# A grouped 3x3 convolution: building the even output bank by accumulation and the odd one from a copy taken in between

## The chip, the cores and the metric

The kernel runs on one core of a Trainium2 chip. Its time is the device time of one execution in microseconds, the median over several runs. Beside it stands one execution recorded by the hardware profiler, from which all views of the profile come. The engines are written as in the profile: PE is TensorE (matrix products; its weight loads are listed apart as PEld), DVE is VectorE, ACT is ScalarE, POOL is GpSimd, SP is the queue that issues most DMAs.

## The reference

The input x has 160 images of 128 channels and 32 x 32 positions. Each image is group-normalised (32 groups of 4 channels), convolved with a 3x3 kernel of 128 x 128 channels, and added to itself. There are five sets of weights; 32 images use each. The weights are U quantised on two levels with steps taken from the range of the whole of U.

```python
beta, alpha = jnp.max(U), jnp.min(U)
s1 = (beta - alpha) / 3.0
v1 = s1 * floor(U / s1)
s2 = s1 / 5.0
v2 = s2 * floor((U - v1) / s2)
w = (v1 + v2).reshape(OUT_CH * 5, IN_CH, 3, 3)
# x viewed as (32, 5 * 128, 32, 32), five groups, padding 1
out = x + conv(group_norm(x), w, feature_group_count=5)
```

## The kernel before

**The arithmetic.** An output image is held as two PSUM banks of 128 x 512 values, called even and odd: for most purposes the even and the odd rows (or, in images called combined, the even and the odd columns). Two neighbouring outputs of a three-tap filter share work: with taps g0, g1, g2, one product of g0+g1+g2 with a sum of the two inner inputs, and one product of g0-g1+g2 with their difference; half the sum and half the difference of these two products are the shared parts of the two outputs. So an image needs four groups of products: SUM weights with the sums (quarter 2 of the prepared input), DIFF weights with the differences (quarter 3), and one group each with the outer taps for the even and the odd bank (quarters 0 and 1). Inputs are fp16, split into a high and a low part for accuracy. A *combined* image has all quarters in both parts (tiles `vh` and `vl`, 128 x 2048, 24 products of up to 512 columns). Another image takes its high part by the plain taps (18 products of tile `hi`) and only its low part by quarters (tile `rows`, 12 products). `combined` decides which image is of which kind: every second one up to image 29, then three of five, then three of four.

**The path of one image through the engines.** `sums_of_pairs` (L854) lets PE make the DIFF products in the bank `m2_ps` and the SUM products in `m1a` or `m1b`. `leave` (L888, its instruction is L891) lets ACT copy half of `m2_ps` to SBUF, tile `m`. `pairs` (L894) lets DVE write the even bank as half of m1 plus m (L903), and the odd bank as half of m1 minus m (L905). `main` (L878) lets PE add the remaining products to the even bank (a = 0) and to the odd bank (a = 1). `residual` (L921) then copies both banks, in one ACT instruction of 1024 columns (L929), to a tile `sum`, which a DMA of POOL's queue adds to the output in memory (L953). The first three and the last four images are finished by DVE instead (L946).

**What is prepared ahead.** ACT measures each image in two passes (L241, L248; eight images are measured by DVE), makes `vh` (L738) or `hi` (L648), and for some images `z` (L640). DVE makes `vl` (L744) or `lo` and `rows` (L751, L764, L772, L773), and in `combine` a part of the tile `v` (L690, L697). POOL makes the rest of `v` (L678, L708) or `z` (L714); `beside_pairs` ties its start to an instruction of DVE in the same step, so that it runs beside `pairs`. The weights of the next set are quantised on DVE in small pieces (class `Later`, L142 to L162, L549) strewn between these.

**The order.** Everything is ordered by hand, in `run`: a program of 160 steps, in which each engine's instructions are queued in the order of the calls. In step i, `conv(i)` queues on PE `sums_of_pairs(i + 1)`, then `main(i, 0)` and `main(i, 1)`. ACT gets: the first pass of new measurements, `residual(i - 1)`, `leave(i + 1)`, the high part of an image further on, the second pass. DVE gets: the low part of image i+2 (from step 14 on of image i+3; in step 13 both images 15 and 16), `pairs(i + 1)`, `combine` of image i+4 (later i+5), measurements. Images 0 to 2 are done by plain taps; step 3 (`FIRST`) is the first of the regular ones. `FURTHER` is 11.

**PSUM.** [...] two pairs for even and odd (`ps_eo`), `m1a`, `m1b`, `m2_ps`, and one for small things.

## Time and profile before

| | |
|---|---|
| median of three runs | 966.45 us (965.62 to 966.77) |
| the profiled execution, its time | 964.56 us |
| its span, first to last instruction | 962.5 us |
| PE busy | 927.8 us, 4432 products |
| DVE busy | 902.6 us |
| ACT busy | 862.7 us |
| POOL busy | 460.1 us |
| mean granted PE clock | 0.995 |

The profiled execution took 2.1 us more than its span, and 1.9 us less than the median. "Busy" is the time in which at least one instruction of the engine was under way. Rows of the view by line give the count, the busy time, the mean duration of one instruction, and after the second bar the idle time of the engine just before these instructions with what ended it. The mean duration of a product (375 ns) is longer than the spacing of products, which overlap; from the starts in the timeline, a product of 512 columns follows the one before after 0.21 us. The page's chain of work that ended last is empty for this run, so that the waits have to be read from the view of waits and the timeline.

### The profile page before, as it was taken

The numbers are of one execution on the slowest core, as the hardware profiler recorded it, in microseconds if no ns is written. First come the engines' busy times: TensorE is split into PE (matmuls) and PEld (weight loads), VectorE is DVE, ScalarE is ACT, GpSimd is POOL, SyncE is SP. The second block draws the span as 40 slices with busy tenths as digits, with TensorE's granted clock in tenths as the row PEclk, the third lists the DMA queues.
The fourth block names the chain that finished last, engine by engine and source line by source line (L and its number), as shares of the span: only waits on it lengthen the run. The fifth ranks groups of instructions, "written<-read, shape, count | busy, mean of one in ns | idle before, by whom it ended". The sixth has DMA issues, their size and how long they took to land.

```text
span 962.5 us, 13034 instructions
## 1 busy us (share of the span) xinstructions
PE 927.8 (96%) x4432; PEld 433.8 (45%) x4432; DVE 902.6 (94%) x1269; ACT 862.7 (90%) x1167; POOL 460.1 (48%) x477
## 2 busy tenths in 40 slices
PE   2899989999999999999999999999999999999997
PEld 1344434444444444444444444444444444444443
DVE  7989999999899999989999999899999998999993
ACT  5879989999899999999999999999999999997660
POOL 4344434456445445554545445545444366565640
PEclk9999999999999999999999999999999999999999
DMA  9079999999999999999999999999999999856563
GB/s 349 36 267 345 334 348 320 325 321 325 328 321 323 317 295 308 272 306 254 295 251 289 284 293 297 282 277 286 267 273 267 282 279 269 172 91 107 91 107 112
DMA packets 67450, 254.22 MB, mean 264 GB/s; under 512 B 5296, under 2 KB 5296, under 8 KB 67376
## 3 DMA queue, kind: packets, MB, share of 16 engines
q1 hardware_dynamic: 45344, 173.09, 48.0%
q0 software_dynamic: 22032, 80.23, 44.4%
q8 instruction: 36, 0.59, 0.2%
q14 instruction: 38, 0.31, 0.1%
HBM read 89.19 MB, written 164.10 MB: 263 GB/s over the span
## 4 chain that ended last, share of the span: by engine, by line


## 5 line engine op out<-in xcount | busy, mean ns | idle before, releaser
L788 PE MATMUL eo<-hi,wt 128*128 128x496 f16 (+3 forms) x1170 | 310.8, 376 | 2.4 <-DVE eo L905 1.7
L843 PEld LDWEIGHTS <-wt 128*128 128x128 f16 x1884 | 183.9, 99 | 211.5 <-DVE eo L905 2.7
L744 DVE SCALAR_TENSOR_TENSOR vl<-v,rstd,vh 128x2048 f16<-128x2048 f32 x94 | 221.8, 2360 | 0.2 <-ACT vh L738 0.2
L843 PE MATMUL eo<-vh,wt 128*128 128x512 f16 x561 | 210.1, 375 | 1.2 <-DVE eo L905 1.2
L843 PE MATMUL eo<-vl,wt 128*128 128x512 f16 x561 | 210.1, 374 | 0.0
L738 ACT ACTIVATE vh<-v,rstd 128x2048 f16<-128x2048 f32 x94 | 188.2, 2002 | 4.8 <-DVE v L697 4.3
L929 ACT COPY sum<-eo 128x1024 f32<-128x1024 f32 x153 | 161.0, 1052 | 32.3 <-PE eo L843 31.7
L788 PEld LDWEIGHTS <-wt 128*128 128x128 f16 x1242 | 121.2, 99 | 142.8 <-DVE eo L905 4.9
L678 POOL TENSOR_SCALAR v<-xt,ngm 128x64 f32<-128x64 f32 x94 | 79.1, 842 | 202.0 <-DVE vl L744 86.9
L248 ACT ACTIVATE junk<-xt,mv 128x1024 uint8<-128x1024 f32 x152 | 174.4, 1148 | 0.3
L241 ACT ACTIVATE junk<-xt 128x1024 uint8<-128x1024 f32 x152 | 160.5, 1056 | 13.3 <-DMA xt<-in_x_dram 10.0
L714 POOL TENSOR_SCALAR z<-xt,ngm,rstd 128x1024 f32<-128x1024 f32 x49 | 93.3, 1904 | 165.1 <-DVE rows L773 55.0
L843 PEld LDWEIGHTS <-across 128*128 128x128 f16 x1128 | 110.8, 98 | 131.9 <-issue 4.9
L843 PE MATMUL eo<-rows,wt 128*128 128x512 f16 x378 | 143.5, 380 | 0.0
L953 POOL DMA_DIRECT2D out_dram<-sum x153 | 133.7, 874 | 14.4 <-ACT sum L929 6.6
L690 DVE TENSOR_TENSOR v<-xt 128x960 f32<-128x960 f32 x94 | 114.0, 1212 | 0.0
L843 PE MATMUL m<-vl,across 128*128 128x496 f16 (+1 forms) x282 | 106.4, 377 | 2.1 <-DVE vl L744 2.1
L891 ACT ACTIVATE m<-m 128x512 f32<-128x512 f32 x157 | 93.7, 597 | 14.1 <-PE m L843 13.7
L843 PE MATMUL m<-vh,across 128*128 128x496 f16 (+1 forms) x282 | 106.2, 376 | 0.2 <-ACT m L891 0.2
L708 POOL TENSOR_TENSOR v<-xt 128x512 f32<-128x512 f32 x94 | 97.2, 1034 | 0.0
L751 DVE TENSOR_TENSOR lo<-z,hi 128x1024 f16<-128x1024 f32 x66 | 80.6, 1221 | 0.0
L286 POOL TENSOR_TENSOR rstd<-ve,mhalf 128x8 f32<-128x8 f32 (+2 forms) x24 | 42.3, 1761 | 65.1 <-DVE rows L773 21.1
(150 smaller groups left out, 1166.3 us busy)
## 6 DMA issues: line engine op xcount, KB each, us to landing
xt<-in_x_dram SPq DMA_DIRECT2D x78, 1024.0 KB, 9.6
out_dram<-sum POOLq DMA_DIRECT2D x153, 512.0 KB, 8.7
out_dram<-xt SPq DMA_DIRECT2D x76, 1024.0 KB, 14.2
out_dram<-xt SPq DMA_DIRECT2D x7, 512.0 KB, 3.3
u<-in_L_conv_U_dram SPq DMA_DIRECT2D x4, 576.0 KB, 13.6
xt<-in_x_dram SPq DMA_DIRECT2D x4, 512.0 KB, 10.1
range<-in_L_conv_U_dram SPq DMA_DIRECT2D x3, 576.0 KB, 8.3
u<-in_L_conv_U_dram SPq DMA_DIRECT2D x2, 288.0 KB, 3.1
```

Source lines behind the costliest of these rows:

```text
L241: self.nc.scalar.activation(junk, image, ACTF.Copy, scale=-1.0 / image.shape[1], accum_out=self.mv[:, j, 0:1],)
L248: self.nc.scalar.activation(junk, image, ACTF.Square, bias=self.mv[:, j, 0:1], accum_out=self.mv[:, j, 1:2],)
L690: nc.vector.tensor_tensor(self.view(v, 1, (511, 2), (half, H), (1, half - 1)), self.view(x, 1, (1, 2), (W, H), (2, half - 1)), self.view(x ...
L708: ins = nc.gpsimd.tensor_sub(self.v[i][:, 1536:], odd, even)
L714: ins = nc.gpsimd.tensor_scalar(z, self.image(i), st.ngm[:, j], st.rstd[:, j], ALU.add, ALU.mult)
L738: self.nc.scalar.mul(vh, self.v[i], st.rstd[:, j])
L744: yield self.nc.vector.scalar_tensor_tensor(vl, self.v[i], st.rstd[:, j], self.hi[i], ALU.mult, ALU.subtract)
L788: nc.tensor.matmul(self.bank(target, a)[:, first:end, c0:c1], self.wts[n, col][:, k, :], tile[:, s0 : s0 + 2 * (end - first) - 1 : 2, c0 + ...
L843: self.nc.tensor.matmul(out, weights, moving, start=start and j == 0, stop=False, skip_group_check=True)
L891: self.nc.scalar.mul(m2, self.m2_ps, 0.5)
L929: nc.scalar.copy(self.as_banks(i, self.sum[i]), self.flat(i, eo))
L953: added = self.nc.gpsimd.dma_start(self.ov[n, :, b], self.sum.pop(i), accum_op=ALU.add)
```

## The change

The four pieces of an output pair are put together in another way. PE makes the SUM products directly in the image's even bank (`begin`). ACT copies that bank to SBUF, tile `half` (`leave`, now L906, a plain copy). PE then adds the DIFF products to the same bank (`complete`), which so becomes the sum of both. DVE makes the odd bank alone: twice the copy minus the even bank (`odd_from_even`, L913). For the factors to fit, SUM and DIFF weights are halved when they are made (one more instruction each time), and LIFT, a scale that weights and inputs share, is halved.

Even and odd banks come from pools of their own, four and three banks; m1a, m1b and m2_ps are gone. `residual` copies the two banks with two ACT instructions of 512 columns (L941), and in the images finished by DVE adds them with two instructions (L955).

The order of the calls changes too. In the steady steps (from step 15) PE's queue is `complete(i + 1)`, `begin(i + 2)`, `main(i, 0)`, `main(i, 1)`, and ACT gets `leave(i + 2)` at the place where it had `leave(i + 1)`. In steps 4 to 14 PE's queue is `begin(i + 1)`, `main(i, 0)`, `complete(i + 1)`, `main(i, 1)`, and ACT gets `leave(i + 1)` ahead of all else in the step. In step 14 `begin(16)` and a second `leave` come in addition. In step 3 `complete(4)` comes last; `complete(3)` stands behind the last plain taps of step 2, just ahead of `main(3, 0)`. The numbers of products are the same as before. `main(i, 0)` adds to the bank that `odd_from_even(i)` reads, so it waits for that instruction, as it waited for `pairs(i)`.

```diff
-LIFT = 2.0**14
+LIFT = 2.0**13
...
-        self.ps_eo = pool("ps_eo", 2, space=PSUM)
-        ps_m = pool("ps_m", 1, space=PSUM)
+        self.ps_even = pool("ps_even", 4, space=PSUM)
+        self.ps_odd = pool("ps_odd", 3, space=PSUM)
...
         yield engine.tensor_tensor(total, g0, g2, ALU.add)
+        yield engine.tensor_tensor(total, total, g1, ALU.add)
+        yield engine.tensor_scalar_mul(total, total, 0.5)
         yield engine.tensor_tensor(diff, total, g1, ALU.subtract)
-        yield engine.tensor_tensor(total, total, g1, ALU.add)
...
-    def sums_of_pairs(self, i):
-
-        for quarter, kind, target in (
-            (3, self.DIFF, self.m2_ps), (2, self.SUM, self.m1(i))
-        ):
-            for step in self.KS:
-                self.product(target, i, quarter, step, kind, start=step == self.KS[0])
+    def begin(self, i):
+
+        even = self.bank_of(self.ps_even, i)
+        self.eo[i] = [even]
+        for step in self.KS:
+            self.product(even, i, 2, step, self.SUM, start=step == self.KS[0])
+
+    def complete(self, i):
+
+        for step in self.KS:
+            self.product(self.eo[i][0], i, 3, step, self.DIFF)
+
+    def steady(self, i):
+
+        return i > self.FURTHER + 2
...
-        if self.FIRST < i < self.imgs - 1:
-            self.sums_of_pairs(i + 1)
-        if i == self.FIRST:
+        ahead = range(i + 1, self.imgs)[:1]
+        if self.steady(i) and self.steady(i - 1):
+            for k in ahead:
+                self.complete(k)
+            for k in range(i + 2, self.imgs)[:1]:
+                self.begin(k)
+            self.main(i, 0, lambda: on_the_way(self.COLS[1]))
+            self.main(i, 1, lambda: on_the_way(self.COLS[2]))
+        elif i == self.FIRST:
             self.main(i, 0)
-            self.sums_of_pairs(i + 1)
+            self.begin(i + 1)
             on_the_way(self.COLS[1])
             self.main(i, 1)
             on_the_way(self.COLS[2])
+            self.leave(i + 1)
+            self.complete(i + 1)
         else:
+            self.begin(i + 1)
             self.main(i, 0, lambda: on_the_way(self.COLS[1]))
+            self.leave(i + 1)
+            self.complete(i + 1)
+            if self.steady(i):
+                self.begin(i + 2)
             self.main(i, 1, lambda: on_the_way(self.COLS[2]))
...
-        m2 = self.evac.tile([self.P, self.H // 2, self.W], F32, tag="m2", name=f"m2_{i}")
-        self.nc.scalar.mul(m2, self.m2_ps, 0.5)
-        self.m2[i] = m2
+        half = self.half[i] = self.evac.tile(
+            [self.P, self.H // 2, self.W], F32, tag="half", name=f"half{i}"
+        )
+        self.nc.scalar.copy(half, self.eo[i][0])
...
-        nc.vector.scalar_tensor_tensor(even, m1, 0.5, m2, ALU.mult, ALU.add)
-        between()
-        nc.vector.scalar_tensor_tensor(odd, m1, 0.5, m2, ALU.mult, ALU.subtract)
+        even, odd = self.eo[i][0], self.bank_of(self.ps_odd, i)
+        self.eo[i].append(odd)
+        self.nc.vector.scalar_tensor_tensor(
+            odd, self.half.pop(i), 2.0, even, ALU.mult, ALU.subtract
+        )
...
-            nc.scalar.copy(self.as_banks(i, self.sum[i]), self.flat(i, eo))
+            image = self.as_banks(i, self.sum[i])
+            for a in range(2):
+                nc.scalar.copy(image[:, a], self.flat(i, eo[a]))
...
                 if i == self.FIRST - 1:
-                    self.sums_of_pairs(self.FIRST)
+                    self.begin(self.FIRST)
+                    self.leave(self.FIRST)
...
+                if i == self.FIRST - 1:
+                    self.complete(self.FIRST)
...
-                if i + 1 < self.imgs:
-                    self.leave(i + 1)
+                if self.steady(i) and i + 2 < self.imgs:
+                    self.leave(i + 2)
...
                 if i + 1 < self.imgs:
-                    self.pairs(i + 1)
+                    self.odd_from_even(i + 1)
```

More of the change, by code (lines that the diff above doesn't have):

```diff
@@ L455, in __init__ @@
         self.small = pool("small", 3)
-        self.ps_eo = pool("ps_eo", 2, space=PSUM)
-        ps_m = pool("ps_m", 1, space=PSUM)
+        self.ps_even = pool("ps_even", 4, space=PSUM)
+        self.ps_odd = pool("ps_odd", 3, space=PSUM)
         ps_small = pool("ps_small", 1, space=PSUM)
         self.steps = Steps(nc, keep)
-        self.m1a, self.m1b, self.m2_ps = (
-            ps_m.tile([P, self.H // 2, self.W], F32, tag=name, name=name)
-            for name in ("m1a", "m1b", "m2")
-        )
-        self.pair = [self.m1a, self.m2_ps]
         small = ps_small.tile([P, 512], F32, tag="small", name="small")
         self.pt, self.pg = small[:, : ROW * P].rearrange("p (k o) -> p k o", k=ROW), small[:, ROW * P :]
-        self.chunks, self.z, self.hi, self.v, self.eo, self.m2 = {}, {}, {}, {}, {}, {}
+        self.chunks, self.z, self.hi, self.v, self.eo, self.half = {}, {}, {}, {}, {}, {}
         self.sum, self.stored = {}, {}
         self.tables, self.wts, self.across = {}, {}, {}
-        self.columns = []
+        self.columns, self.warm = [], None
         cuts = [0, 2, 4, 8, 12, 16, 20, *range(24, self.imgs + 1, 8)]
@@ L524, in over_partitions @@
         nc, P = self.nc, self.P
-        place = self.bank_pair("range").rearrange("p h r w -> p h (r w)")
-        rows = place[0:1, 0, : 2 * P].rearrange("p (k c) -> p k c", k=2)
+        place = [self.bank_of(pool, "range").rearrange("p r w -> p (r w)") for pool in (self.ps_even, self.ps_odd)]
+        rows = place[0][0:1, : 2 * P].rearrange("p (k c) -> p k c", k=2)
         for k in range(2):
@@ L532, in over_partitions @@
         nc.vector.tensor_reduce(top, rows, AX.X, ALU.max)
-        spread = place[:, 1, :2]
+        spread = place[1][:, :2]
         nc.tensor.matmul(spread, self.ones, top, start=True, stop=True)
@@ L788, in taps @@
                 nc.tensor.matmul(
-                    self.bank(target, a)[:, first:end, c0:c1],
+                    target[a][:, first:end, c0:c1],
                     self.wts[n, col][:, k, :],
@@ L795, in taps, with bank_of @@
                 )
-    def bank_pair(self, i):
-        return self.ps_eo.tile([self.P, 2, self.H // 2, self.W], F32, tag="eo", name=f"eo{i}")
-    def bank(self, target, h):
-        return target[h] if isinstance(target, list) else target[:, h]
+    def bank_of(self, pool, name):
+        tag = "even" if pool is self.ps_even else "odd"
+        return pool.tile([self.P, self.H // 2, self.W], F32, tag=tag, name=f"{tag}{name}")
     def warm_up(self, count):
         zeros = self.los[3].rearrange("p h w -> p (h w)")
+        if self.warm is None:
+            self.warm = self.bank_of(self.ps_odd, "warm")
         for _ in range(count):
             self.nc.tensor.matmul(
-                self.pair[0].rearrange("p i w -> p (i w)"), zeros[:, :128],
+                self.warm.rearrange("p i w -> p (i w)"), zeros[:, :128],
                 zeros[:, :512], start=True, stop=True,
@@ L815, in direct_hi @@
         if i not in self.eo:
-            self.eo[i] = self.bank_pair(i) if i < 2 else self.pair
+            self.eo[i] = [self.bank_of(pool, i) for pool in (self.ps_even, self.ps_odd)]
         self.taps(i, (self.hi[i], 0), col, self.eo[i])
@@ L845, in product @@
             )
-    def m1(self, i):
-        return self.m1b if i % 2 else self.m1a
     def both(self, i):
         return ([self.hi[i]] if self.combined(i) else []) + [self.v[i]]
-    def sums_of_pairs(self, i):
-        for quarter, kind, target in (
-            (3, self.DIFF, self.m2_ps), (2, self.SUM, self.m1(i))
-        ):
-            for step in self.KS:
-                self.product(target, i, quarter, step, kind, start=step == self.KS[0])
-    def conv(self, i, on_the_way):
-        if self.FIRST < i < self.imgs - 1:
-            self.sums_of_pairs(i + 1)
-        if i == self.FIRST:
+    def begin(self, i):
[8 more added lines that the diff above has]
+        return i > self.FURTHER + 2
+    def conv(self, i, on_the_way):
+        ahead = range(i + 1, self.imgs)[:1]
[7 more added lines that the diff above has]
+        elif i == self.FIRST:
             self.main(i, 0)
-            self.sums_of_pairs(i + 1)
+            self.begin(i + 1)
             on_the_way(self.COLS[1])
@@ L878, in main @@
     def main(self, i, a, between=lambda: None):
-        to = self.bank(self.eo[i], a)
+        to = self.eo[i][a]
         for step in self.KS:
@@ L888, in leave, with odd_from_even @@
     def leave(self, i):
-        m2 = self.evac.tile([self.P, self.H // 2, self.W], F32, tag="m2", name=f"m2_{i}")
-        self.nc.scalar.mul(m2, self.m2_ps, 0.5)
-        self.m2[i] = m2
-    def pairs(self, i, between=lambda: None):
-        nc = self.nc
-        m1, m2 = self.m1(i), self.m2.pop(i)
-        eo = self.eo[i] = self.bank_pair(i)
-        if i == self.imgs - 1:
-            eo = self.eo[i] = [eo[:, 0], self.m1(i - 1)]
-        even, odd = (self.bank(eo, a) for a in range(2))
-        nc.vector.scalar_tensor_tensor(even, m1, 0.5, m2, ALU.mult, ALU.add)
-        between()
-        nc.vector.scalar_tensor_tensor(odd, m1, 0.5, m2, ALU.mult, ALU.subtract)
+        half = self.half[i] = self.evac.tile(
+            [self.P, self.H // 2, self.W], F32, tag="half", name=f"half{i}"
+        )
+        self.nc.scalar.copy(half, self.eo[i][0])
+    def odd_from_even(self, i):
+        even, odd = self.eo[i][0], self.bank_of(self.ps_odd, i)
[3 more added lines that the diff above has]
+        )
     def as_banks(self, i, image):
@@ L911, in as_banks, with flat @@
         return image.rearrange("p (i a w) -> p a i w", a=2, w=self.W)
-    def flat(self, i, banks):
-        return banks.rearrange("p a i w -> p a (i w)") if self.combined(i) else banks
+    def flat(self, i, bank):
+        return bank.rearrange("p i w -> p (i w)") if self.combined(i) else bank
     def by_hand(self, i):
@@ L941, in residual @@
         image = self.as_banks(i, xj)
-        if eo is self.pair:
-            for a in range(2):
-                nc.vector.tensor_add(image[:, a], self.bank(eo, a), image[:, a])
-        else:
-            nc.vector.tensor_add(image, self.flat(i, eo), image)
+        for a in range(2):
+            nc.vector.tensor_add(image[:, a], self.flat(i, eo[a]), image[:, a])
         self.store(i)
@@ L1027, in run @@
             self.measure(i)
-        first_means = self.bank_pair("means").rearrange("p h r w -> p h (r w)")
+        first_means = [self.bank_of(pool, "means").rearrange("p r w -> p (r w)") for pool in (self.ps_even, self.ps_odd)]
         spread = self.over_partitions(
-            ext1, ident, lambda: self.stats_of(0).means(first_means[:, 0])
+            ext1, ident, lambda: self.stats_of(0).means(first_means[0])
         )
@@ L1064, in run @@
         measure(1, 3)
-        self.stats[1].means(first_means[:, 1])
+        self.stats[1].means(first_means[1])
         self.stats[1].deviations()
@@ L1173, in run @@
                 if i == 2:
-                    self.leave(3)
                     self.normalise(5)
@@ L1177, in run @@
                     self.high_part(5)
-                    self.pairs(3)
+                    self.odd_from_even(3)
                     self.low_part(4)
```

## The prediction, made before the changed kernel ran

> **What bounds the kernel now.** I began with the engines' totals on the page and the busy time in stretches of 40 us (columns: stretch, then busy us and count for PE, PEld, DVE, ACT, POOL, then granted clock, DMA share, GB/s).

> ```profile
> PE 927.8 (96%) x4432; PEld 433.8 (45%) x4432; DVE 902.6 (94%) x1269; ACT 862.7 (90%) x1167; POOL 460.1 (48%) x477
> ```

> ```profile
> 80.00:120.00 40.00, 40.00 (x199) 19.33 (x198) 39.39 (x67) 38.52 (x56) 15.12 (x17) 1.00 1.04 333
> 120.00:160.00 40.00, 36.05 (x161) 15.79 (x160) 39.55 (x64) 36.27 (x50) 13.38 (x15) 0.96 1.04 337
> 160.00:200.00 40.00, 40.00 (x194) 18.85 (x193) 39.66 (x57) 37.54 (x54) 20.20 (x25) 1.00 1.05 325
> 320.00:360.00 40.00, 40.00 (x195) 18.82 (x193) 38.48 (x53) 39.72 (x55) 18.59 (x18) 1.00 1.05 309
> 840.00:880.00 40.00, 40.00 (x192) 18.68 (x191) 38.17 (x41) 39.70 (x53) 23.23 (x22) 1.00 0.63 99
> ```

> About 194 products per 40 us are one per 0.206 us. Only 120:160 falls short, with 161. So PE's stream sets the time, and only its halts can be won. The waits of PE, and the timeline around the greatest, show them (time, duration, engine, instruction; in brackets idle time before it and who ended it):

> ```profile
> PE m L843 <- DVE vl L744: 2.1, 1, 2.1
> PE eo L788 <- DVE eo L905: 1.7, 2, 1.0
> PE eo L843 <- DVE eo L905: 1.2, 3, 0.5
> PE m L843 <- DVE rows L773: 0.8, 1, 0.8
> PE m L843 <- ACT m L891: 0.2, 1, 0.2
> ```

> ```profile
> 127.43 0.38 PE L843 MATMUL m<-vh,across 128*128 128x512 f16 x1 [0.19 <-ACT m L891]
> 129.88 0.59 PE L843 MATMUL m<-vl,across 128*128 128x512 f16 x1 [2.08 <-DVE vl L744]
> ...
> 131.09 0.62 PE L843 MATMUL m<-vh,across 128*128 128x496 f16 x1
> ...
> 131.50 0.62 PE L843 MATMUL m<-vl,across 128*128 128x496 f16 x1
> ...
> 134.63 0.81 PE L788 MATMUL eo<-hi,wt 128*128 128x512 f16 x3 [0.70 <-DVE eo L905]
> ```

> Here PE waits for DVE's `vl`, goes on at half rate, and waits again for the odd bank of image 14. From 126.86 to 134.63, 7.77 us, it starts 13 products, which take 2.8 us elsewhere: 5.0 us are lost. Read in the same way after 55 us: 0.9 at 65.9 (low part late), 0.4 before that, 1.1 at 157.4, 0.4 at 268, 0.6 at 495, 0.7 at 722, 0.2 at 772 (odd bank late). Sum 9.3, of which 9.0 wait for DVE or follow from it. The first 55 us and the end, from 955 us, are not touched by the change.

> [...] 131.09 to 131.50 is 0.41 us, and the lines above end 3.4 us later at full rate. So two microseconds of halt can cost 1.7 us more. [...]

> **The change, part by part.** The groups by line, shapes apart:

> ```profile
> L929 ACT COPY sum<-eo 128x1024 f32<-128x1024 f32 x153 | 161.0, 1052 | 32.3 <-PE eo L843 31.7
> L891 ACT ACTIVATE m<-m 128x512 f32<-128x512 f32 x157 | 93.7, 597 | 14.1 <-PE m L843 13.7
> L903 DVE SCALAR_TENSOR_TENSOR eo<-m1b,m 128x512 f32<-128x512 f32 x79 | 54.7, 692 | 16.4 <-PE m1b L843 11.9 <-ACT m L891 4.5
> L905 DVE SCALAR_TENSOR_TENSOR eo<-m1b,m 128x512 f32<-128x512 f32 x78 | 54.5, 699 | 2.7
> ```

> PE: both programs have the same TensorE instructions in number and size. Nothing.

> DVE loses one of two instructions per image: 157 x 0.73 (the spacing of L903 and L905) = 115 us of busy time. Taken from an engine that isn't the bound, it is worth only the halts that DVE causes. The new operand places (SBUF and PSUM read, PSUM written) are those of L903; I take its 0.70.

> ACT's `leave` stays at 0.60. The residual's copy becomes two: by mean durations 2 x 597 - 1052 = 142 ns more, 22 us in all; by spacing (L891 to the next start 0.485 us, L929 0.96) 0.01 us, 1.5 us in all. Back to back, spacing counts; I take 0.01. ACT has 32.3 + 14.1 us idle before these very lines, which hides it; without that cover, where ACT is at 39.7 of 40, it would be up to 0.14 per image. Seven additions by DVE are split likewise and hidden. The halving of weights is 8 more DVE pieces of some 0.35 us (L573's size) and four on POOL, which delay the first `z` by 0.2 us beside PE's taps: nothing. LIFT: nothing.

> Steady steps, from 15 on. `main(i, 0)` waits for `odd_from_even(i)` where it waited for `pairs(i)`, and DVE gets there 0.7 us sooner. The five halts at 157 and later (1.1, 0.4, 0.6, 0.7, 0.2) are each close to or below that, and `odd_from_even` needn't wait for `leave` of its own step. Gain 3.0. `begin(i + 2)` needs the low part a step sooner than before, but DVE makes it ahead of the odd bank that the next `main` waits for anyway. `leave` must end before the next step's `complete`, the same deadline as before for m2_ps; there one wait of 0.2 is seen. It can start 0.6 to 1.3 us later, since `begin` now follows `complete`; then ACT's idle time before L891 grows. DVE's odd bank stands behind it, with a step to spare.

> Steps 3 to 14, where 6.3 us are lost today. Here I walked along the queues with the rows' durations (a product group 0.64, or 1.28 if combined; half a main 2.55, or 1.27):
> - `main(3, 0)` follows `complete(3)` at once, and the odd bank lies between: 0.27 for the end of the product to be seen (942.24 to 943.16 less three spacings), 0.70, 0.06. One halt of 1.0, new; behind it on DVE stands low part 4, which `begin(4)` needs. Low parts 4 and 5 end about as late as today.
> - `leave(i + 1)` stands first in ACT's step, so it can't run ahead with measurements while `begin` is under way. In step 9 ACT has two images to measure, a `z` and a `hi`: 7.4 us. `leave(11)` then ends some 5.5 us into step 10, where `complete(11)` could start at 3.8: a halt of 1.6 to 1.9. The same after step 12 (7.5 us): 1.5 in step 13. Everything on PE stands behind these.
> - Image 14's odd bank. In step 13 DVE has two low parts to make; today it ends at 134.6. Taking 0.73 from each of five steps gives 131.0. But DVE, too, now waits for the late `complete`s, and in steps with `combine` for POOL's part of `v`:

> ```profile
> 150.56 1.03 POOL L708 TENSOR_TENSOR v<-xt 128x512 f32<-128x512 f32 x1
> ...
> 150.98 0.70 DVE L905 SCALAR_TENSOR_TENSOR eo<-m1b,m 128x512 f32<-128x512 f32 x1
> ...
> 151.59 1.15 DVE L690 TENSOR_TENSOR v<-xt 128x960 f32<-128x960 f32 x1
> ```

> L690 starts where POOL's L708 ends; without one of the two instructions before it DVE would stand still for most of those 0.7 us. With all such waits I get 135.6. Moreover `complete(15)`, 1.28, comes after this halt, where its products came before it. So the stretch gains 134.6 - 131.0 - 1.3 = 2.3, or loses 135.6 - 134.6 + 1.3 = 2.3. I take the middle, nothing: the halts change their place and their cause.

> Sum: 3.0 of gain against the profiled run's 964.56 (span 962.5 and 2.1 around it), so 961.6. The median shown is 1.9 higher, and I predict 966.45 - 3.0 = 963.4.

> **The rivals.** *All of DVE's halts go.* For: DVE is the named releaser of 9.0 us, and loses 13% of its work. Against: the two ACT deadlines and POOL's `v`. 966.45 - 9.0 = 957.4, and nearer 959 with the new 1.0 in step 3.
> *Slower: ACT's copy in mid-step becomes PE's wait.* Its place is `complete` in steps 5 to 14, with ACT at 38.5 of 40 us and the step's ACT work uneven (3.6 to 7.5 us). Price: the 2.3 above, and a half-rate window, 1.7, after each of two halts, and two more halts of some 1.2: 8.1 against 3.0, so 966.45 + 5.1 = 971.5. It decides the sign once the ramp loses more than 3.0. Against: a halt of 1.1 at 157 left the clock alone.
> *The relief is eaten by POOL.* DVE waits at L690 for what it saved, in 94 combined images, and the odd bank comes as late as before: 966.0, no change. Against: the odd bank itself still comes before L690 in the queue.

> **How the numbers follow.** This kernel's measurement can tell some 0.2%, 1.9 us, from no change. My forecast (964.9 to 961.0 as its own range) has 0.45, full relief 0.27, slower 0.18, eaten by POOL 0.10. Faster by over 0.2% (below 964.5): 0.34 of the first and the second, 0.61; slower 0.17 (little of the last case falls below the bound); the rest, 0.22, is the same. For 8 in 10 the range reaches from 958.5, inside full relief, to 968.0, partly into the slower case, which takes in both ends of the ramp and of the copy's price.

> **What would show it.** Right: DVE near 790 us busy, ACT within 10 us of 863; PE's waits for L913 after 150 us gone; halts before `complete` ended by ACT L906 in steps 10 and 13, one of 1 us before `main(3, 0)`, and one at about 133 us for image 14. Wrong: PE at full count in every stretch after 60 us (full relief), or the clock under 1.00 in more than one stretch between 90 and 140 us, or ACT-ended waits after 200 us.

## The result, and the profile after

The changed kernel took 971.01 us (median of five runs, 970.17 to 972.69), the kernel before 966.68 beside it (965.62 to 967.44): a ratio of 1.0049, with 0.0034 to 0.0063 above one as its 95% interval. It is slower by 4.3 us where 963.4 was forecast, outside the range (958.5 to 968.0), and close to the rival "slower" (971.5). The profiled execution took 971.01 us, with a span of 969.3; that of before, 964.56 with a span of 962.5, was some 2 us faster than its kernel's median, so the two spans differ by 6.8 us where the medians differ by 4.3.

First the totals on the page of the kernel after.

```profile
PE 929.8 (96%) x4432; PEld 435.2 (45%) x4432; DVE 856.0 (88%) x1125; ACT 864.7 (89%) x1320; POOL 447.7 (46%) x481
```

ACT grew by 2.0 us. DVE fell by 46.6 us and not by the 115 of the forecast: something gave more than half of the removed work back.

Busy time in stretches of the kernel after (columns as before: stretch, busy us and count of PE, PEld, DVE, ACT, POOL, granted clock, DMA share, GB/s):

```profile
80.00:120.00 40.00, 37.97 (x185) 17.94 (x183) 34.27 (x58) 37.07 (x59) 15.35 (x18) 1.00 1.04 335
120.00:160.00 40.00, 34.24 (x154) 15.43 (x153) 34.92 (x55) 32.47 (x51) 11.60 (x14) 0.91 1.04 347
320.00:360.00 40.00, 40.00 (x194) 18.79 (x193) 36.36 (x47) 39.84 (x61) 18.51 (x18) 1.00 1.00 276
800.00:840.00 40.00, 39.35 (x188) 18.23 (x186) 35.44 (x34) 37.35 (x58) 16.12 (x20) 1.00 0.91 231
```

PE starts 185 products in 80:120, where it started 199, and 154 in 120:160, where it started 161; the clock there is 0.91 and not 0.96. In 320:360 it is at full count as before. Near 800 a little is missing that was not missing before.

The waits of PE in the kernel after (total us, times, longest):

```profile
PE even L838 <- ACT half L906: 5.1, 6, 1.8
PE even L783 <- DVE odd L913: 3.8, 3, 2.8
PE even L838 <- DVE vl L739: 1.7, 1, 1.7
```

Before, from 55 us on, all but 0.2 us of PE's waits was put down to DVE. The greatest is now ACT's copy. The timeline of the kernel after shows the places (time, duration, instruction; idle time before it and its releaser in brackets):

```profile
110.50 0.38 PE L838 MATMUL even<-vh,across 128*128 128x512 f16 x1 [1.83 <-ACT half L906]
...
133.71 0.38 PE L838 MATMUL even<-vl,across 128*128 128x512 f16 x1 [1.70 <-DVE vl L739]
...
137.72 1.41 PE L783 MATMUL even<-hi,wt 128*128 128x512 f16 x3 [2.80 <-DVE odd L913]
...
821.16 0.38 PE L838 MATMUL even<-vh,across 128*128 128x512 f16 x1 [0.65 <-ACT half L906]
```

The first is `complete(11)` in step 10. At 129.59 `complete(14)` waits 1.27 us for ACT in the same way; then the low part of image 15 is late, then the odd bank of image 14, and then the products go at half rate up to 142 us: the three products of the third shown line take 1.41 us, where three take 0.81 elsewhere. The last shown line is one of three waits for ACT's copy, near 820, 843 and 865 us.

From the starts of the products, less their usual spacing, the time lost between 55 and 155 us is 13.5 us after and 6.4 before; from 155 us on it is 2.7 after and 3.0 before. The sum explains the 6.8 us between the traces. So the first steps lost 7.1 us, and the steady steps won the 3.0 that was forecast there, at 157 us and later, and lost almost all of it again to new waits.

### The profile page after: what moved, and what is told of

The parts are those of the page before. It is cut to its first block, busy times and chain, and to the rows that moved or that the text cites. A ratio compares the mean times of both kernels' runs of the same rounds, so it can differ in the third digit from the quotient of the medians.

```text
span 969.3 us, 13017 instructions
## 1 busy us (share of the span) xinstructions
PE 929.8 (96%) x4432; PEld 435.2 (45%) x4432; DVE 856.0 (88%) x1125; ACT 864.7 (89%) x1320; POOL 447.7 (46%) x481
## 4 chain that ended last, share of the span: by engine, by line
PE 82%; ACT 9%; DVE 5%; issue 3%; DMA 1%; POOL 0%; ACTq 0%; DVEq 0%; POOLq 0%; SPq 0%
PE even L838 43%; PE odd L838 14%; PE even L783 12%; PE odd L783 12%; ACT vh L733 2%; ACT junk L248 2%; ACT sum L941 1%; ACT junk L241 1%; ACT half L906 1%; DMA xt<-in_x_dram 1%; DVE ext L507 1%; DVE ext L508 1%; ACT z L635 1%; DVE lo L746 1%; ACT hi L643 0%
## 5 line engine op out<-in xcount | busy, mean ns | idle before, releaser
L739 DVE SCALAR_TENSOR_TENSOR vl<-v,rstd,vh 128x2048 f16<-128x2048 f32 x94 | 232.5, 2473 | 43.5 <-ACT vh L733 43.3
L838 PE MATMUL even<-vh,across 128*128 128x512 f16 x564 | 211.3, 375 | 3.7 <-ACT half L906 3.7
L838 PE MATMUL even<-vl,across 128*128 128x512 f16 x564 | 211.3, 375 | 1.7 <-DVE vl L739 1.7
L248 ACT ACTIVATE junk<-xt,mv 128x1024 uint8<-128x1024 f32 x152 | 175.8, 1156 | 0.3
L838 PE MATMUL even<-rows,wt 128*128 128x512 f16 x567 | 174.1, 381 | 1.6 <-ACT half L906 1.5
L783 PE MATMUL even<-hi,wt 128*128 128x496 f16 (+3 forms) x594 | 163.6, 380 | 4.8 <-DVE odd L913 3.8
L783 PE MATMUL odd<-hi,wt 128*128 128x496 f16 (+3 forms) x594 | 161.8, 376 | 0.0
L685 DVE TENSOR_TENSOR v<-xt 128x960 f32<-128x960 f32 x94 | 154.7, 1646 | 1.6 <-POOL v L673 1.6
L906 ACT COPY half<-even 128x512 f32<-128x512 f32 x157 | 93.3, 594 | 50.5 <-PE even L838 42.5
L913 DVE SCALAR_TENSOR_TENSOR odd<-half,even 128x512 f32<-128x512 f32 x157 | 108.0, 688 | 22.7 <-PE even L838 19.5
L838 PE MATMUL even<-vh,wt 128*128 128x496 f16 (+1 forms) x282 | 105.6, 375 | 0.0
L838 PE MATMUL even<-vl,wt 128*128 128x496 f16 (+1 forms) x282 | 105.6, 375 | 0.0
L838 PE MATMUL odd<-vl,wt 128*128 128x496 f16 (+1 forms) x282 | 105.6, 374 | 0.0
L838 PE MATMUL odd<-vh,wt 128*128 128x496 f16 (+1 forms) x282 | 105.6, 374 | 0.0
```

What stands on the lines that cost most here:

```text
L248: self.nc.scalar.activation(junk, image, ACTF.Square, bias=self.mv[:, j, 0:1], accum_out=self.mv[:, j, 1:2],)
L685: nc.vector.tensor_tensor(self.view(v, 1, (511, 2), (half, H), (1, half - 1)), self.view(x, 1, (1, 2), (W, H), (2, half - 1)), self.view(x ...
L739: yield self.nc.vector.scalar_tensor_tensor(vl, self.v[i], st.rstd[:, j], self.hi[i], ALU.mult, ALU.subtract)
L783: nc.tensor.matmul(target[a][:, first:end, c0:c1], self.wts[n, col][:, k, :], tile[:, s0 : s0 + 2 * (end - first) - 1 : 2, c0 + dw : c1 + dw],
L838: self.nc.tensor.matmul(out, weights, moving, start=start and j == 0, stop=False, skip_group_check=True)
L906: self.nc.scalar.copy(half, self.eo[i][0])
```

## The experiments

Each kernel ran beside the kernel before, whose medians were 966.4 to 966.6 us. The theory: the loss is in the first steps, where `complete` waits for an ACT copy and DVE is late by more than a step's saving, with a second, smaller loss where the steady order gives ACT less time for its copy. The rival: the new arrangement itself is dearer everywhere, for instance by ACT's divided copies.

### The order in the steady steps

```diff
-            for k in ahead:
-                self.complete(k)
             for k in range(i + 2, self.imgs)[:1]:
                 self.begin(k)
+            for k in ahead:
+                self.complete(k)
             ...
```

> The changed kernel (971.0 us) with one edit: in the steady steps begin(i + 2) stands ahead of complete(i + 1), so that ACT can start its copy 0.6 to 1.3 us sooner and PE needs it as much later. Theory (the three halts of 0.7 to 0.8 us before complete at 820, 843 and 865 us, and three of 0.1 us, come from the copy's late start): they vanish, ACT's idle time before L906 falls from 50 us by a third or more, and the time is 968.3 (967.8 to 969.5); the ramp up to 145 us stays as it is. Rival (ACT is simply overloaded there, by the residual's copy in two instructions): the halts stay, 970.5 to 971.5.

Measured: 968.81 us (ratio to before 1.0026, 1.0018 to 1.0034), so 2.2 us of the loss. These are the waits of the kernel with `begin` first:

```profile
PE even L838 <- ACT half L906: 3.3, 3, 1.8
DVE vl L739 <- ACT vh L733: 19.0, 22, 1.8
ACT half L906 <- PE even L838: 25.0, 23, 7.3
```

And these are the same of the changed kernel:

```profile
DVE vl L739 <- ACT vh L733: 43.3, 40, 3.1
ACT half L906 <- PE even L838: 42.5, 33, 7.1
```

With `begin` behind `complete`, the even bank is ready later in the step; ACT stands idle in front of its copy for 42.5 us in all, everything behind it on ACT is late, and DVE waits 43.3 us for `vh`. None of this stops PE until about 800 us, where three quarters of the images are combined and ACT has no room left; there the copy itself comes 0.7 to 0.8 us late, three times. With `begin` first, those three waits are gone, as the theory said; the three that remain belong to the first steps.

### The first steps as before

Images 3 to 15 are put together as in the kernel before, in the new pools: the DIFF products in the odd bank at the head of the step, copied by ACT behind the residual, and two DVE instructions. From image 16 on all is as changed.

```diff
...
+        if self.apart(i):
+            (even, odd), half = self.eo[i], self.half.pop(i)
+            self.nc.vector.scalar_tensor_tensor(odd, even, 1.0, half, ALU.mult, ALU.subtract)
+            self.nc.vector.scalar_tensor_tensor(even, even, 1.0, half, ALU.mult, ALU.add)
+            return
...
```

> The changed kernel, but images 3 to 15 are put together as in the kernel before, in the new pools: DIFF products go to the image's odd bank at the head of the step, ACT copies that bank at its old place behind the residual, and DVE makes both banks with two instructions; from image 16 on all is as in the changed kernel. Theory (the loss lies in the order of steps 3 to 14): the halts up to 145 us fall from some 13.5 us to the 7 of before, and the time is 965.5 to 967. Rival (the loss comes from what holds in all steps, the two copies of the residual or the late start of the copy): 970 or more.

Measured: 966.99 us (ratio 1.0002, 0.9994 to 1.0010): 4.0 us come back. The loss between 55 and 155 us is 9.0 in its trace, and the three waits near 820 to 865 us are still there.

Both edits together:

> Both edits, begin ahead of complete in the steady steps and images 3 to 15 put together as before. Theory: the gains add, 962.8 to 964.8, faster than the kernel before by 2 to 4 us; what is left of halts after 55 us is some 6 to 7 us up to 145 us and below 0.5 us after it. Rival (the ramp's loss is only put off, and comes back where the two schemes meet at image 16): no better than the kernel before, 966 to 968.

Measured: 965.01 us (ratio 0.9984, 0.9977 to 0.9992). The two parts add: 2.2 + 4.0 = 6.2 from the changed kernel, 6.0 measured. What is left of the change without its two losses is a gain of 1.6 us (0.8 to 2.2 by the interval). The rival falls: what may be dearer in every step costs less than the change gains there.

### ACT's load in the first steps

ACT's measurements of images 12 to 27 read 128 of an image's 1024 values, so the statistics of these images are not the reference's.

```diff
+        if 12 <= i < 28:
+            image = image[:, :128]
...
```

> The changed kernel, but the statistics that ACT takes of images 12 to 27 read 128 of their 1024 values (so the output is not the reference's): ACT loses some 1.7 us per such image and step in the ramp, and the order stays. Theory (ACT's copy, queued first in its step behind an uneven load of measurements, is what PE waits for at 108 and 128 us, and it also delays DVE): both halts vanish, the halts at 132 and 135 us shrink by 1 to 2 us together, and the time is 965 to 968. Rival (DVE's two low parts of step 13 set the end of the ramp whatever ACT does): PE waits longer at 132 to 137 us instead, 969.5 or more.

Measured: 967.77 us (ratio 1.0011, 1.0005 to 1.0018), 3.2 us less than the changed kernel. The waits of PE in the kernel with light measurements:

```profile
PE even L840 <- DVE vl L741: 1.9, 1, 1.9
PE even L785 <- DVE odd L915: 3.8, 3, 2.8
```

Both waits for ACT in steps 10 and 13 are gone: PE is at full count in 80:120. But PE still waits 1.9 us for the low part of image 15 and 2.8 us for the odd bank of image 14, where the theory had these two halts shrink; the time came into its range without that. The odd bank itself came sooner, as this line of the same kernel shows beside the one at 137.72 us above:

```profile
133.02 0.99 PE L785 MATMUL even<-hi,wt 128*128 128x512 f16 x2 [2.80 <-DVE odd L915]
```

That is 4.7 us sooner. Only 1.1 us of it was there at `main(3, 0)` already (58.72 us here, 59.80 in the changed kernel). So the late `complete`s had held up DVE, too, as the prediction said: in the changed kernel DVE waits 0.7 us for `complete(11)`, 1.5 for a late `vh` and 1.3 for a late piece of ACT's between 110 and 130 us, and here none of this. PE comes sooner by as much, and what is left of the two halts is DVE's own work: from 100 to 133 us it has one wait, of 0.3 us.

### DVE's double step

In step 13 DVE makes two low parts, of images 15 and 16, and then the odd bank of image 14. Here the odd bank stands between them:

```diff
                 for k in self.step_of(i, 2):
+                    if k == self.FURTHER + 5:
+                        self.odd_from_even(i + 1)
...
-                if i + 1 < self.imgs:
+                if i + 1 < self.imgs and i != self.FURTHER + 2:
                     self.odd_from_even(i + 1)
```

> The changed kernel with one thing moved: in step 13 DVE makes the odd bank of image 14 between its two low parts (of images 15 and 16) and not behind both. Theory (the halt of 2.96 us before main(14, 0) is DVE's second low part standing ahead of the odd bank, and with the two halts before it, it brings the half-rate window of 2.3 us): that halt shrinks below 0.5 us and the window goes, 971.0 - 2.5 - 2.3 = 966.2, between 965.5 and 967.5. Rival (DVE is short of time there whatever the order): the low part of image 16 comes late instead, a halt of 2 to 3 us before begin(16), and the time stays between 969.5 and 971.5.

Measured: 968.50 us (ratio 1.0019, 1.0013 to 1.0026), 2.5 us less; between theory (966.2) and rival. The stretch and a wait of this kernel:

```profile
120.00:160.00 40.00, 35.27 (x170) 16.27 (x168) 36.21 (x57) 36.08 (x55) 13.76 (x13) 1.00 1.04 349
```

```profile
PE even L838 <- DVE rows L767: 1.7, 1, 1.7
```

The halt of 2.96 and the half-rate window are gone (clock 1.00, 170 products where there were 154), but a later low part stops PE by 1.7 us, and by smaller amounts at 149 and 161 us. A debt of DVE was moved, not paid.

### What slowed DVE

The view by line showed another surprise. First L690 of the kernel before, then the same line (now L685) after, both 128 x 960 (count, busy us, mean ns, idle before):

```profile
L690 DVE TENSOR_TENSOR v<-xt 128x960 f32<-128x960 f32 x94 | 114.0, 1212 | 0.0
```

```profile
L685 DVE TENSOR_TENSOR v<-xt 128x960 f32<-128x960 f32 x94 | 154.7, 1646 | 1.6 <-POOL v L673 1.6
```

Its instruction is unchanged, and it takes 434 ns more in the mean, 41 us in all. The mean hides two kinds: 71 of the 94 take over 1.3 us, and POOL's L703 runs beside each of them; the 20 without L703 beside them take 1.15 to 1.17. The timeline of the kernel after shows one of the slow kind:

```profile
125.12 1.03 POOL L703 TENSOR_TENSOR v<-xt 128x512 f32<-128x512 f32 x1
125.42 1.76 DVE L685 TENSOR_TENSOR v<-xt 128x960 f32<-128x960 f32 x1
```

L685 has two inputs in SBUF, POOL ends at 126.15, and 0.6 of the 0.7 us between 125.42 and that time are what L685 takes beyond its 1.15. Before, POOL's 1.03 us lay beside the two instructions of `pairs`, which read one input from PSUM and show 0.69 to 0.70 us in the mean with POOL's L708 beside them, and 0.70 where no instruction of POOL is beside them (15 cases); one of the two is gone. To see whether it is the cause, POOL's instruction was put behind `combine`:

```diff
...
         nc.vector.scalar_tensor_tensor(
             v[:, 1024:1536], even, st.twice[:, j], odd, ALU.add, ALU.add
         )
+        done = self.last_of_vector()
+        self.after(nc.gpsimd.tensor_sub(v[:, 1536:], odd, even), done)
...
-            even, odd = (self.image(i)[:, a::2] for a in range(2))
-            ins = nc.gpsimd.tensor_sub(self.v[i][:, 1536:], odd, even)
+            return
...
```

> The changed kernel with POOL's tensor_tensor on v (L703) queued behind DVE's two instructions of combine for the same image, so that the two engines no longer work on v side by side. Theory (DVE's L685, 1646 ns in the mean after the change, is slow because L703 runs beside it): L685 falls to 1150 to 1250 ns, and DVE's busy time from 856 to between 810 and 825 us, unless the next vl, now beside L703, takes some of it. Rival (L685 is slow for what ACT or the DMAs read): it stays above 1550 ns and DVE above 845 us. Both expect the time within 1.5 us of the changed kernel's 971.0, since DVE is not what PE waits for in the steady steps.

Measured: 971.93 us (ratio 1.0055, 1.0040 to 1.0071). Two groups of this kernel:

```profile
L696 POOL TENSOR_TENSOR v<-xt 128x512 f32<-128x512 f32 x94 | 194.1, 2064 | 89.1 <-DVE v L692 89.1
L685 DVE TENSOR_TENSOR v<-xt 128x960 f32<-128x960 f32 x94 | 108.6, 1156 | 5.7 <-POOL v L673 5.7
```

L685 is at 1156 ns: the cause is shown. But DVE's busy time is 852.4, only 3.6 less; that part of the expectation missed, and in a telling way. POOL's instruction now meets `vl` and the low parts, and it is held (2064 ns in the mean), or it holds what DVE starts next, or both, as here in the timeline of this kernel:

```profile
268.17 3.07 POOL L696 TENSOR_TENSOR v<-xt 128x512 f32<-128x512 f32 x1 [1.11 <-DVE v L692]
270.26 1.20 DVE L146 TENSOR_TENSOR k<-nnn,lt 128x384 f16<-128x384 int16 x1
```

L146 takes 0.35 us when alone; the first of the `rows` instructions of a low part went from 686 to 914 ns in the mean. In this order POOL's 1.03 us per combined image costs DVE nearly as much as beside `combine`; beside the pair of the kernel before, whose instructions have one SBUF input each, it cost little (1212 ns for L690, where 1150 is the time alone).

### Mending the first steps, and spending what DVE has won

These kernels start from the one of 965.01 us. First, DVE makes the low part of image 16 behind the pair of image 14, and measures image 24 a step later, out of the way of the low part of image 15.

> The kernel with the first steps put together as before and begin ahead of complete (965.0 us), in which DVE makes the low part of image 16 behind the pair of image 14, and measures image 24 at the end of step 13 and not of step 12, ahead of the low part of image 15. Theory (the halt of 2.6 us at 128.8 is the low part of image 15 standing behind that measurement of 1.7 us, and the half-rate window follows from it): 965.0 - 1.7 - 1.5 = 961.8, between 961 and 963.2. Rival (DVE is behind by the whole step, and what is moved comes late at the next place): 964 to 965.5.

Measured: 963.94 us (ratio 0.9968, 0.9956 to 0.9980), between theory and rival. In the profiled execution the wait for the low part of image 15 fell from 2.6 to 0.9 us, and at 143 us one of 3.0 came up for a later low part, with a half-rate window: what was moved came late at the next place, as the rival said. That execution was the slowest of six (962.3 to 966.5), so the others may have lost less there. In the next kernel DVE makes no piece of the next weights in steps 11 to 14:

```diff
-            later.next_image()
+            if not 11 <= i <= 14:
+                later.next_image()
...
-                        36 / (self.per_set - 6 - b),
+                        36 / (self.per_set - 6 - b - 4 * (n == 0)),
```

> The kernel with mended first steps (963.9 us) in which DVE makes no piece of the next weights in steps 11 to 14; they are made up for in the other steps up to 28. Theory (the halts left there, 0.9 at 129.6 and 3.0 with its half-rate window of 1.7 at 143.4, come from a debt of DVE of about one low part, 3 to 4 us, and four steps of weights, some 1.2 us each, pay it): those halts go, 963.9 - 5.6 = 958.3, between 957.5 and 961. Rival (the debt lies in the order of the steps, not in DVE's load): above 962.5.

Measured: 961.10 us (ratio 0.9942, 0.9928 to 0.9955), just above the theory's range and short of its 958.3 by 2.8. The half-rate window went and the greatest halt shrank to 1.9 us, but two of 1.0 us stand at 91 and 102 us, where there were 0.4 and 0.2. So DVE's load is a good part of the debt; not all of it was paid.

Then the time that DVE has to spare in the steady steps was spent on taking products off PE. `combined` chooses more of images 30 to 129:

```diff
-        return i % 5 % 2 == 0 if i < self.THIRDS else i % 4 != 2
+        return i % 16 not in (2, 5, 9, 12, 15) if i < self.THIRDS else i % 4 != 2
...
-        return i in self.BY_VECTOR
+        return i in self.BY_VECTOR or i >= 40 and i % 16 == 3
```

> A try at a faster version: the kernel with the first steps put together as before and begin ahead of complete (965.0 us), in which 69 instead of 60 of images 30 to 129 are combined and seven more images are measured by DVE. Theory (PE's products are the bound, and DVE's freed time can be spent): 9 x 6 products fewer, 9 x 1.27 = 11.4 us, so 953.6, between 952.5 and 956. Rival (ACT, 97% busy there with one more us per combined image, or DVE with two more, becomes the bound): 959 or above, with PE's waits ended by ACT's half or DVE's odd bank between 200 and 800 us.

Measured: 967.81 us (ratio 1.0012, 1.0005 to 1.0019), slower than its base. The rival named the right kind of end, with another wait, as PE's waits in this kernel show:

```profile
PE even L838 <- DVE vl L739: 12.9, 16, 1.6
```

DVE is at 77.7 to 78.0 of 80 us in most stretches from 320 to 800, ACT mostly at 75 to 76. Without the added measurements:

> 69 instead of 60 of images 30 to 129 combined, as in the run with more combined images, but on the kernel of 965.0 us without the seven measurements added to DVE. Theory (that run's halts of 17 us waiting for the low part vl came from DVE at 97% of every stretch; the seven measurements of 1.8 us brought it there, and ACT, at 94%, can take them back): of the 11.4 us of products saved at most 3 are lost to new halts, 953.6 to 957. Rival (two more us of DVE in each added combined image are too much by themselves, with POOL's work on v slowing them): 961 or above, with PE again waiting for vl.

Measured: 959.55 us (ratio 0.9931, 0.9916 to 0.9946); between theory and rival; 8.0 us are still lost after 155 us, where the theory allowed 3. Together with the mended first steps:

> The last two together. If their effects lie in different stretches (before 150 us, and 200 to 800 us) they add: by the two theories 958.3 - 11.4 + 3 at most, 947 to 951. If either theory falls, its part is missing: 953 to 959 with one, above 961 with neither.

Measured: 955.61 us (ratio 0.9891, 0.9876 to 0.9906): 5.5 less than 961.10, as 959.55 is 5.5 less than 965.01, so the two add. It is above the 947 to 951 of the two theories, since each run had gained less than its theory said. The greater halts, of 1.1 to 1.5 us, came every 90 us, once in 16 images. Last, the pattern was changed to two of every three images:

```diff
-        return i % 16 not in (2, 5, 9, 12, 15) if i < self.THIRDS else i % 4 != 2
+        return i % 3 != 2 if i < self.THIRDS else i % 4 != 2
```

> The fastest version so far (955.6 us) with two of every three images from 30 to 129 combined (67 in all) and never three in a row, where it had 69, with three in a row once in 16. Theory (its halts of 7.7 us after 200 us, the largest 1.1 to 1.5 every 90 us, come where DVE has three combined images in a row): two images fewer cost 2.5 us, and of the 7.7 at least 5 go, 951.5 to 953.5. Rival (DVE's mean load, 97%, makes the halts, wherever the images stand): as many halts per image of DVE's load, 955 to 958.

Measured: 952.01 us (951.8 to 952.5; ratio 0.9851, 0.9837 to 0.9864), the fastest of all, 14.5 us below the kernel before. A stretch of it:

```profile
320.00:400.00 80.00, 80.00 (x389) 37.74 (x387) 76.59 (x101) 79.46 (x121) 36.55 (x38) 1.00 1.05 317
```

DVE and ACT are both nearly full, and PE does not stop: 0.6 us are lost after 155 us. The time is within the theory's range. Two things changed together, the pattern and DVE's load in this stretch (77.7 of 80 before, 76.6 now), so that the unevenness is the likelier cause of the halts and not one shown alone.

## Why the prediction was wrong

**Failed: "I take the middle, nothing."** This is the term for steps 3 to 14. The walk's parts were nearly all seen: 1.0 before `main(3, 0)`; 2.0 at `complete(11)` (1.6 to 1.9 said); 1.4 at `complete(14)` (1.5 said), both ended by ACT's copy, which stood behind measurements; then the odd bank of image 14. But this bank was there at 137.7 us, and the walk's two ends were 131.0 and 135.6. Taking the middle between a gain and a loss stood in for an answer that the walk already leant to; the bank came 2.1 us past the worse end. The half-rate window, 2.3 us after the halts, was in the rival's price and not in the sum. The term was 0 and is 7.1 us between the traces; undoing the change in these steps alone gives 4.0 of it back in the medians. Of this, two causes are shown, each by a run: ACT's measurements ahead of the copy (3.2 us when made light; the half-rate window stayed) and DVE's second low part ahead of the odd bank (2.5 us when the order is turned; the window went). The two edits did not run together, so how far they add is open.

**Failed: the delayed start of `leave` costed at nothing.** The prediction saw that it "can start 0.6 to 1.3 us later", and named the deadline as unchanged. But a later start with the same deadline takes 0.6 to 1.3 us from ACT's room, and ACT had 0.3 of 40 us idle in 840:880. It cost 2.2 us, by waits ended by ACT after 200 us, one of the signs that the prediction had set down for being wrong.

**Wrong size: DVE's busy time, "near 790 us".** It was 856.0. The prediction saw L690 start where POOL's instruction ends, counted an idle wait there only for the first steps, and called the case in which POOL eats the relief a rival. The wait showed as a longer L685, 41 us in all. In the steady steps it cost PE nothing, since DVE stands idle there anyway (43.3 us for `vh` and 19.5 for PE in all); in the first steps it is part of the debt, how much was not separated. Of the other 27 us of the missing saving, `vl` took 11 (2473 ns in the mean, 2360 before). Another 11 lie in how the saving was counted: by their durations the pair's instructions take 110 us less and not 115, and DVE's instructions overlap each other by 7 us less than before (70.4 us in all, 77.2 before). The rest lies in small pieces, the halvings (2) among them.

**Right: the steady gain, and the copy's price.** All five halts at 157 us and later went, and no wait for L913 is left after 150 us. The net gain without the two losses was 1.6 us and not 3.0 by the medians; in the traces the steady steps gained 2.4 (3.0 lost before, 0.6 with both edits). The difference lies within the 2 us by which the profiled run of before was faster than its median, and no trace here can settle it. ACT's divided copy cost 2.0 us of busy time against 1.5 said: spacing, not duration, was the right measure (`sum` at 95.48 and 96.00, the next start 96.50). The separate durations would have said 22. The pace of PE's stream held, too (389 products in 80 us in the fastest version, 0.206 each). The waits of `complete` for ACT's copy (5.1 us in all) and of `main` for the odd bank (3.8) follow from the program: the products change the very values that the copy and DVE's instruction read.

**The rivals.** "Slower: ACT's copy in mid-step becomes PE's wait" is what happened in the first steps, at its price (971.5) by partly other means: it had 8.1 against 3.0, the traces show 7.1 and 2.7 against 3.0. It was given 0.18 although the prediction's own walk had found both of its halts. The argument against it, that a halt of 1.1 at 157 left the clock alone, spoke of a single halt, and here three stood within 10 us. "Full relief" fails by these halts. "Eaten by POOL" was right on the mechanism, and wrong on what it costs.

## What to carry to other kernels

When a walk along the queues finds a new wait on the path, put it into the sum, with the window of slow clock that may follow when several waits stand close together (6.83 us at half rate in the changed kernel); a middle between two ends is not a forecast. A copy that moves into the middle of a step turns every uneven step of its engine into a halt of the bound engine: look at the engine's heaviest step, and at the room left where it is fullest, not at its mean. Time freed on an engine that is not the bound is worth what it can take off the bound: here some 1.6 us by itself, and, spread evenly over more combined images with the first steps mended, 14.5. How much of the 14.5 the kernel before would have gained by the same choices was not run: the mending of the first steps, some 4 us of it, eases steps that are put together as before.

## What the runs showed of the hardware that was not expected

In these runs POOL and DVE held each other up where both inputs of DVE's instruction lie in SBUF, and in both directions: L685 took 1.15 to 1.17 us in the 20 cases without L703 beside it and 1.81 in the mean of the 71 slow ones, 1.76 beside POOL's 1.03 in the lines shown above; L690 of the kernel before took 1.99 in the six cases that lay beside L708; POOL's instruction took 1.03 alone and up to 4.4 us when it stood behind `combine`. In the trace the engine that is held looks busy, not idle (L685 is busy for 154.7 us, L690 was for 114.0), so the view of waits doesn't show it: a mean that grew without a change of the instruction does.

```profile
126.27:129.68 3.41, 1.34 (x6) 0.45 (x7) 3.34 (x6) 3.41 (x4) 0.00 (x0) 1.00 1.06 334
129.68:133.09 3.41, 3.21 (x8) 1.17 (x8) 3.41 (x7) 3.36 (x7) 0.14 (x1) 0.50 1.03 347
```

In the kernel after it followed after the one stretch with 2.20 us and after no other, the next in size having 1.83:

```profile
108.31:111.72 3.41, 1.58 (x8) 0.67 (x7) 3.07 (x6) 3.38 (x8) 0.62 (x1) 1.00 1.04 346
111.72:115.14 3.42, 3.42 (x20) 1.72 (x18) 1.64 (x3) 3.42 (x4) 1.62 (x2) 1.00 1.03 328
132.20:135.61 3.41, 1.21 (x5) 0.48 (x5) 3.41 (x4) 3.09 (x6) 0.00 (x0) 1.00 1.02 327
135.61:142.44 6.83, 4.72 (x12) 1.72 (x12) 4.93 (x7) 2.00 (x4) 4.18 (x5) 0.50 1.03 422
```

So a halt of 1.8 us at 108 us in the kernel after cost only itself, and the halts of 1.7 and 2.8 us at 132 to 137.7 brought 6.83 us at half rate, since 2.2 us of them fell into 132.20 to 135.61. The grid lies elsewhere in each of these executions. The kernel with the first steps as before and `begin` first, and the one with more combined images, have the same halt of 2.4 us ending at 131.60. In the first, 1.5 us of it fell into one stretch, which with 0.5 of an earlier halt makes 1.99, and the clock was at half for 6.83 us. In the second the grid cut it at 130.25, neither stretch had more than 1.6, and the clock was at full rate in both:

```profile
127.28:130.70 3.42, 1.43 (x7) 0.73 (x8) 3.32 (x8) 3.42 (x7) 0.00 (x0) 1.00 1.05 367
130.70:137.53 6.83, 5.93 (x15) 2.13 (x15) 6.83 (x10) 3.86 (x9) 2.17 (x2) 0.50 1.03 366
```

```profile
126.84:130.25 3.41, 1.85 (x9) 0.73 (x8) 3.31 (x12) 3.41 (x6) 0.00 (x0) 1.00 1.04 386
130.25:133.66 3.41, 2.06 (x10) 0.97 (x10) 3.41 (x4) 3.41 (x8) 0.00 (x0) 1.00 1.03 283
```

Half rate followed 1.99, 2.07 and 2.20 us, and not 1.83 or 1.56. A forecast of such a halt can give the window a chance, and not a certainty.
